# A graph network on one core: indirect fetches that name only the rows a slot can use, in steps of 32

## The chip, the cores and the metric

The kernel runs on one core of a Trainium2 chip. The time is device microseconds of one execution; the figure given for a kernel is the median of several runs. Before the change it is 6249.97 us (three runs: 6262.89, 6249.97 and 6209.29 us).

The engines appear under these names: PE multiplies matrices (PEld loads its weights), DVE is the vector engine, ACT the scalar engine with its activation functions, POOL the general engine, which also issues every indirect DMA here, and SP issues plain DMAs. Each engine runs its own list of instructions in order, and the lists wait for one another through semaphores.

## What is computed

The reference is a chain of eight layers on 3125 nodes with 256 features: four graph layers, each followed by a layer on single nodes. The edge list has 53125 entries (25000 random pairs in both directions and one loop for each node), sorted by destination, so that a node has 17 incoming edges on average. Cut to its frame:

```python
edge_index = jnp.stack([src, dst])
x = x + _L0_gnn_ref(_layernorm(x, axis=-1), edge_index, ...)      # two attention layers
x = x + _L0_ffn_ref(_layernorm(x, axis=-1)[None], ...)[0]
x = x + _L1_gnn_ref(edge_index, _layernorm(x, axis=-1), edge_type_8, ...)   # relational sum
x = x + _L1_ffn_ref(_layernorm(x, axis=-1)[None], ..., L1_ffn_edge_index)[0]  # experts, gates by a graph
x = x + _L2_gnn_ref(_layernorm(x, axis=-1), ...)
x = x + _L2_ffn_ref(_layernorm(x, axis=-1)[None], ...)[0]
x = x + _L3_gnn_ref(_layernorm(x, axis=-1), ..., edge_attr_3, edge_index)   # attention with edge attributes
x = x + _L3_ffn_ref(_layernorm(x, axis=-1)[None], ...)[0]
```

An attention layer computes a score for each edge from the rows of its two nodes, takes a softmax over the edges that enter a node, and adds the source rows with these weights:

```python
m = xl[src] + xr[dst]
logits = jnp.einsum('ehc,hc->eh', jax.nn.leaky_relu(m, NEG_SLOPE), att)
...
out = jax.ops.segment_sum(alpha[:, :, None] * xl[src], dst, num_segments=n_nodes)
```

The gates of the first expert layer come from a small attention layer on a second random graph of 65536 edges, of which those that enter the 3125 nodes matter.

## The kernel before

**Nodes by degree.** The prologue ranks the nodes by their number of incoming edges, largest first (`by_degree`, L1165), and cuts the ranking into NT = 25 groups of P = 128 nodes, one node to a partition. The edges of a group are handled in slots: slot s of a group holds, for each of its 128 nodes, that node's edge number s. How many slots each group gets is fixed when the program is built: `profile` (L1032) works from a Poisson distribution of the degrees and gives KS = 41, 25, 23, 22, 21, 21, 20, ..., 12, 11, 10, in all TOT = 453 slots. OFF holds the first slot of each group. For the second graph KR is KS less one (428 slots, offsets OFFR), since its loops are handled apart. `by_degree` also compares the counted degrees with limits that it writes with memsets into `least` (L1214); if a limit is passed, a flag sends the kernel into a general version for any graph. The limit at slot KS[g] is that at most 128 x g nodes have more edges.

**The gather stages of `quick` (L1414).** Five stages fetch source rows from a table in HBM. For every slot, POOL issues one indirect DMA (`gather`, L1078): 128 indices, one from each partition, and 128 rows into one slot of a tile `gt`. Where a node has fewer edges than the slot number, the index names some other row, and a penalty of -1e30 on the score (`pen`) makes its weight zero; in the relational sum the index names a row of zeros instead (`relz`).

- T1, T2: two attention layers through `gat` (L1650), with rows of 260 and 257 words. A chunk is C4 = 4 slots in one tile; a group has one slot more, for the node's own row, which ACT copies in (L1670). The steps of a chunk are `fetch`, `own`, `add` (DVE adds the destination rows, L1674, ACT takes Abs, L1675) and `score` (DVE, L1680 to L1682), one turn apart; when a group is through, `weigh` (L1601) takes the softmax and forms weighted rows `wv` (DVE, L1637, in T1; ACT, L1635, in T2), which PE adds with an identity matrix (L1623).
- rel: the relational sum through `plain_sum` (L1693), with rows of 256 words. There are no scores: PE adds the fetched rows as they are (L1708). Beside it DVE and POOL sort the second graph, and call `by_degree` for it (L1974).
- gm: the gates, `gates_by_slots` (L2310), with rows of 32 words; a tile holds all slots of a group. Beside it PE, DVE and ACT work on the experts.
- TA: the attention with edge attributes (fetch at L2766), with rows of 264 words; PE encodes the attributes (`enc_ahead`, L2847, and L2800).

**Order.** `pipeline` (L1088) and `in_turns` (L1578) write the order out by hand: each turn issues up to two fetches, as long as a tile is free (14 in `gat` and TA, 12 in `plain_sum`) and the fetch is no more than `lead` chunks ahead (8; 6 in TA), and then one step of each kind for the chunk whose turn it is. Inside one engine nothing overtakes.

Of the kernel before, what the change touches and what calls it, by code (L numbers as in the profile page):

```python
# [11 lines left out]
F32 = mybir.dt.float32  # L12
# [8 lines left out]
P = 128  # L21
D = 256
KD = D // P
N = 3125
NT = (N + P - 1) // P
NP = NT * P
# [1005 lines left out]
def profile():  # L1032


    mean = (E - N) / N
    p = [math.exp(-mean)]
    for i in range(1, 200):
        p.append(p[-1] * mean / i)
    ks = []
    for g in range(NT):  # L1040
        d = 1
        while True:
            tail = max(1.0 - sum(p[:d]), 0.0)
            c = N * tail
            if (c < 1e-3) if g == 0 else (c + 4.0 * math.sqrt(c * (1.0 - tail)) <= P * g):
                break
            d += 1
        ks.append(d)
    return ks


KS = profile()
OFF = [sum(KS[:g]) for g in range(NT)]
TOT = sum(KS)
DC = KS[0] + 3
# [106 lines left out]
        yield 0  # L1162


def by_degree(tc, k, pool, psum, name, cls, total, slots, record, table, bad):  # L1165

    nc = tc.nc
    R, M = cls.shape[0], cls.shape[1]  # L1170
    cls_f = pool.tile([P, DC], F32, name="cls_f")
    nc.gpsimd.iota(cls_f, pattern=[[1, DC]], base=0, channel_multiplier=0, allow_small_or_imprecise_dtypes=True)
    before = pool.tile([P, P], F32, name="before")
    nc.gpsimd.affine_select(out=before, in_=k.ones, pattern=[[1, P]], compare_op=ALU.is_gt,
                            fill=0.0, base=0, channel_multiplier=-1)
    keep = pool.tile([R, DC, M], F32, name="keep")
    nc.gpsimd.memset(keep, 1.0)
    nc.gpsimd.memset(keep[:, :, 0:1], 0.0)
    S = [R, DC, M]
    oh = pool.tile(S, F32, name="oh0")  # L1180
    nc.vector.tensor_tensor(oh, cls_f[:R, :, None].to_broadcast(S), cls[:, None, :].to_broadcast(S), ALU.is_equal)
    yield 0
    pre = pool.tile(S, F32, name="pre")
    nc.vector.tensor_tensor_scan(pre.rearrange("p c t -> p (c t)"), keep.rearrange("p c t -> p (c t)"),
                                 oh.rearrange("p c t -> p (c t)"), 0.0, op0=ALU.mult, op1=ALU.add)
    tot = pool.tile([R, DC], F32, name="tot")
    nc.vector.tensor_copy(tot, pre[:, :, M - 1])
    yield 0
    cps = psum(2 * DC).rearrange("p (s c) -> p s c", s=2)
    nc.tensor.matmul(cps[:, 0, :], k.ones[:R, :], tot, start=True, stop=True)  # L1190
    nc.tensor.matmul(cps[:, 1, :], before[:R, :], tot, start=True, stop=True)
    yield 0
    cum = pool.tile([R, DC], F32, name="cum")
    nc.vector.tensor_tensor_scan(cum, k.ones[:R, :DC], cps[:R, 0, :], 0.0, op0=ALU.mult, op1=ALU.add)
    bb = pool.tile([R, DC], F32, name="bb")
    nc.vector.scalar_tensor_tensor(bb, cum, -1.0, cps[:R, 1, :], op0=ALU.mult, op1=ALU.add)
    nc.vector.tensor_scalar_add(bb, bb, float(total - 1))
    nc.vector.tensor_add(pre, pre, bb[:, :, None].to_broadcast(S))
    yield 0
    nc.vector.tensor_mul(pre, pre, oh)  # L1200
    rank = pool.tile([R, M], F32, name="rank")
    nc.vector.tensor_reduce(rank, pre.rearrange("p c t -> p t c"), AX.X, ALU.add)
    yield 0
    rank_i = pool.tile([R, M], I32, name="rank_i")
    nc.vector.tensor_copy(rank_i, rank)
    nrec = pool.tile([R, M, 4], F32, name="nrec")
    nrec_i = nrec.bitcast(I32)
    nc.vector.memset(nrec[:, :, 3:], 0.0)
    nc.vector.tensor_copy(nrec_i[:, :, 0], record[0])
    nc.vector.tensor_copy(nrec_i[:, :, 1], record[1])  # L1210
    nc.vector.tensor_copy(nrec[:, :, 2], record[2])
    least = pool.tile([R, DC], F32, name="least")
    nc.gpsimd.memset(least, 0.0)
    for g in range(NT - 1, -1, -1):  # L1214
        nc.gpsimd.memset(least[:, slots[g] + 1 : slots[g] + 2], float(total - P * g))
    over = pool.tile([R, DC], F32, name="over")
    nc.vector.tensor_tensor(over, cum, least, ALU.is_lt)
    nc.vector.tensor_reduce(bad[:R, :], over, AX.X, ALU.add)
    yield 0
    for t in range(M):  # L1220
        scatter(tc, name, table, rank_i[:, t : t + 1], nrec[:, t, :])
        for _ in range(4):
            yield 0
# [54 lines left out]
def prologue(tc, a, k):  # L1278
# [8 lines left out]
    with tc.tile_pool(name="pr", bufs=1) as pr, tc.tile_pool(name="prw", bufs=3) as prw, \  # L1287
# [59 lines left out]
        bad = pr.tile([P, 5], F32, name="bad")  # L1347
        nc.vector.memset(bad, 0.0)
        for _ in by_degree(tc, k, pr, lambda n: prp.tile([P, P], F32, name="s_ps", bufs=2)[:, :n], "perm", cls,
                           NP, KS, (n_f, S[:, :NT], deg), k.perm_d, bad[:, 0:1]):  # L1350
            pass


# [60 lines left out]
def quick(ctx: ExitStack, tc: tile.TileContext, a: dict, out: bass.AP, k):  # L1414
# [16 lines left out]
    slot = q.tile([P, KS[0]], F32, name="slot")  # L1431
    nc.gpsimd.iota(slot, pattern=[[1, KS[0]]], base=0, channel_multiplier=0,
                   allow_small_or_imprecise_dtypes=True)
    zeros = q.tile([P, W1], F32, name="zeros")
    nc.vector.memset(zeros, 0.0)
    zero = zeros[0:1, :D]

# [160 lines left out]
    def all_chunks(own=0):  # L1598
        return [(g, c, n, c + n == KS[g] + own) for g in range(NT) for c, n in chunks(g, own)]

    def weigh(pool, psum, g, L, H, tiles, own=0):  # L1601


        K = KS[g] + own
        by_head = L.rearrange("p k h -> p h k")
        nc.vector.tensor_add(L[:, : KS[g], :], L[:, : KS[g], :],
                             pen[:, OFF[g] : OFF[g] + KS[g], None].to_broadcast([P, KS[g], H]))
        mx = pool.tile([P, H], F32, name="mx")
        nc.vector.tensor_reduce(mx, by_head, AX.X, ALU.max)
        if not own:  # L1610
            nc.vector.tensor_scalar_max(mx, mx, -0.5 * BIG)
        nc.vector.tensor_sub(L, L, mx[:, None, :].to_broadcast([P, K, H]))
        nc.scalar.activation(L, L, AF.Exp)
        yield 0
        den = pool.tile([P, H], F32, name="den")
        nc.vector.tensor_reduce(den, by_head, AX.X, ALU.add)
        acc = psum.tile([P, D], F32, name="acc", bufs=2)
        held = []

        def summed():  # L1620
            for c, n, wv in held:
                for s in range(n):
                    nc.tensor.matmul(acc, ident, wv[:, s, :], start=(c + s == 0), stop=(c + s == K - 1))  # L1623
            held.clear()


        todo = list(zip(chunks(g, own), tiles))
        per = 2 if len(todo) > 6 else 1
        for i in range(0, len(todo), per):
            made = []  # L1630
            for (c, n), t in todo[i : i + per]:
                wv = pool.tile([P, C4, D], F32, name="wv", bufs=4)
                if H == 1:
                    for s in range(n):
                        nc.scalar.activation(wv[:, s, :], t[:, s, :D], AF.Copy, scale=L[:, c + s, 0:1])  # L1635
                else:
                    nc.vector.tensor_mul(wv[:, :n, :].rearrange("p s (h c) -> p s h c", h=H),  # L1637
                                         t[:, :n, :D].rearrange("p s (h c) -> p s h c", h=H),
                                         L[:, c : c + n, :, None].to_broadcast([P, n, H, D // H]))
                made.append((c, n, wv))  # L1640
            summed()
            held.extend(made)
            yield len(made)
        summed()
        weighed[g] = acc, den
        yield 0
# [3 lines left out]
    def gat(H, table, own_rows, att, gp, mp, sp, psum, opened, finish, beside=None):  # L1650
# [5 lines left out]
        def fetch(g, c, n, last):  # L1656
# [3 lines left out]
                        st[a_] = SimpleNamespace(R=own_rows(a_), tiles={})  # L1660
            t = st[g].tiles[c] = gp.tile([P, C4, W], F32, name="gt")
            for s in range(n - last):
                gather(nc, t[:, s, :], table, recs_i[:, OFF[g] + c + s, 0:1])

        def own(g, c, n, last):
            if c == 0:
                opened(g)
                st[g].L = sp.tile([P, KS[g] + 1, H], F32, name="L", bufs=4)
# [24 lines left out]
    def plain_sum(table, idx, gp, psum, start, tail, beside=None):  # L1693
# [3 lines left out]
        def fetch(g, c, n, last):  # L1697
            t = tiles[g, c] = gp.tile([P, C4, D], F32, name="gt")
            for s in range(n):
                gather(nc, t[:, s, :], table, idx[:, OFF[g] + c + s : OFF[g] + c + s + 1])  # L1700

        def add(g, c, n, last):
            if c == 0:
# [1 line left out]
                start(accs[g], g)  # L1705
            t = tiles.pop((g, c))
            for s in range(n):
                nc.tensor.matmul(accs[g], ident, t[:, s, :], start=False, stop=(last and s == n - 1))  # L1708
            return 1

        pipeline(tc, all_chunks(), 12, 8, fetch, (add,), lambda g: tail(g, accs.pop(g)), beside, 4)
# [161 lines left out]
    def route_merge(pool, psum, pieces, G):  # L1873
# [69 lines left out]
        for i in range(4):  # L1943
# [27 lines left out]
        cls = pool.tile([RQ, 25], F32, name="rm_cls")  # L1971
        nc.vector.tensor_scalar(cls, deg, 1.0, float(DC - 1), op0=ALU.add, op1=ALU.min)
        nc.vector.tensor_scalar_max(cls, cls, 0.0)
        yield from by_degree(tc, k, pool, psum, "perm2", cls, N, KR, (ids[:RQ, :], at_f[:, :25], deg), perm2_d,  # L1974
                             bad[:, 2:3])
        ps = psum(5)
        nc.tensor.matmul(ps, ones, bad, start=True, stop=True)
# [332 lines left out]
    def gates_by_slots(gc, gp, sp, beside, pieces):  # L2310
# [23 lines left out]
        def fetch(g):  # L2334
            t = tiles[g] = gp.tile([P, KR[g] + 1, GW], F32, name="gt")
            for i in range(KR[g]):
                gather(nc, t[:, i, :], gm, recs2[:, OFFR[g] + i : OFFR[g] + i + 1])
            nc.scalar.copy(t[:, KR[g], :], own[g])

        def score(g):  # L2340
# [381 lines left out]
    with tc.tile_pool(name="ag", bufs=abufs) as gp, tc.tile_pool(name="am", bufs=2) as mp, \  # L2722
# [43 lines left out]
        def fetch(g, c, n, last):  # L2766
            t = gp.tile([P, C4, WA], F32, name="gt")
            tiles.setdefault(g, []).append(t)
            for s in range(n):
                gather(nc, t[:, s, :], TA, recs_i[:, OFF[g] + c + s, 0:1])  # L2770

        def attrs(g, c, n, last):
            if c % SE == 0:
# [71 lines left out]
                ready[2 - j](*seq[i - 1 - j])  # L2845

        def enc_ahead(g, c, n, last):  # L2847
            i = seq.index((g, c, n, last))
            for j, r in enumerate(ready):
                if i + j < len(seq):  # L2850
# [169 lines left out]
```

## Time and profile before

| | |
|---|---|
| median of three runs | 6249.97 us |
| profiled execution, its own time | 6249.48 us |
| its span, first to last instruction | 6247.7 us |
| mean granted TensorE clock | 0.758 |
| chain that ended last | PE 14%, issue 13%, POOL 5%, DVE 4%, DMA 2% of the span |

The costliest groups that touch the gathers, with their busy time and the mean of one:

| group | count | busy us | mean ns |
|---|---|---|---|
| L1079 POOL indirect DMA, T1 and T2 | 906 | 1013.0 | 1118 |
| L1079 POOL indirect DMA, gm | 428 | 468.1 | 1094 |
| L1079 POOL indirect DMA, TA | 453 | 462.9 | 1022 |
| L1079 POOL indirect DMA, rel | 453 | 441.9 | 975 |
| L1623 PE, adding weighted rows | 2818 | 915.0 | 485 |
| L1708 PE, adding rows in rel | 906 | 324.0 | 490 |
| L1674 DVE, adding destination rows | 258 | 297.1 | 1152 |
| L1675 ACT, Abs | 258 | 256.4 | 994 |

Busy time on POOL is the time in which it prepares the DMA; the data land later. A group's idle time names what the engine waited for before it: "issue" means that the profile shows nothing it waited for. PE adds in fp32 with two passes, so L1708 has two records for each slot. A window of the profile gives the busy time of each engine between two times.

### The profile page before, as it was taken

The page shows a single profiled execution, that of the slowest core. Times are in us where ns is not written, and L with a number is a line of the kernel's source. Part 1 is how long each engine was busy: PE and PEld are TensorE (multiplying, and loading weights), DVE is VectorE, ACT ScalarE, POOL GpSimd, SP SyncE. Part 2 cuts the span into 40 slices and gives each one's busy share as a digit, 9 for nine tenths or more (in the row PEclk, how much of TensorE's full clock was granted, in tenths as well). Part 3 has the DMA queues.
Part 4 walks back from the last instruction along what each step waited for, and adds up shares of the span by engine and source line. Part 5 has one row for each costly group of instructions (what it writes and reads, how often), then busy time and mean ns, then how long its engine had stood idle before and what let it go on. Part 6 is the DMA issues. An engine that isn't in the chain of part 4 may idle for free. (4 is left out here: it accounts for less than half of the span.)

```text
span 6247.7 us, 45320 instructions
## 1 busy us (share of the span) xinstructions
PE 3803.4 (61%) x14067; PEld 2490.4 (40%) x14119; DVE 3126.3 (50%) x6081; ACT 1220.8 (20%) x2574; POOL 3144.9 (50%) x3123
## 2 busy tenths in 40 slices
PE   2344543455598844635286630799695788838885
PEld 1233332333355423424154320465352344426664
DVE  4588878898874345601153324423214677840001
ACT  1222212445622100000043320211021000002221
POOL 3677774667773276675456563210106566631112
PEclk9666766677799956657698765899756777869998
DMA  3533442333312233222243223332242233324444
GB/s 123 142 103 99 108 110 81 94 91 104 91 23 84 112 91 93 78 75 56 60 135 80 57 54 98 105 107 98 71 131 87 78 88 85 89 83 140 159 156 132
DMA packets 356485, 601.24 MB, mean 96 GB/s; under 512 B 109648, under 2 KB 252858, under 8 KB 352898
## 3 DMA queue, kind: packets, MB, share of 16 engines
q0 software_dynamic: 131472, 329.19, 19.7%
q1 hardware_dynamic: 202233, 246.71, 12.3%
q10 hardware_dynamic: 22518, 22.24, 1.1%
q8 instruction: 116, 1.90, 0.1%
q14 instruction: 146, 1.20, 0.1%
HBM read 458.81 MB, written 142.98 MB: 96 GB/s over the span
## 5 line engine op out<-in xcount | busy, mean ns | idle before, releaser
L1623 PE MATMUL acc<-wv,ident 128*128 128x256 f32 x2818 | 915.0, 485 | 601.4 <-ACT wv L1635 259.3
L1079 POOL DMA_INDIRECT gt<-T,recs x906 | 1013.0, 1118 | 354.5 <-issue 247.8
L1623 PEld LDWEIGHTS acc<-wv,ident 128*128 128x128 f32 x2818 | 659.9, 245 | 860.4 <-ACT wv L1635 290.0
L1079 POOL DMA_INDIRECT gt<-TA,recs x453 | 462.9, 1022 | 250.6 <-issue 130.3
L1079 POOL DMA_INDIRECT gt<-gm,recs x428 | 468.1, 1094 | 172.3 <-issue 130.0
L1079 POOL DMA_INDIRECT gt<-rel,relz x453 | 441.9, 975 | 205.9 <-issue 128.2
L1708 PE MATMUL acc<-gt,ident 128*128 128x256 f32 x906 | 324.0, 490 | 207.8 <-issue 163.0
L2569 PE MATMUL acc<-XNT,adj_g 128*128 128x512 bf16 x1198 | 404.1, 386 | 42.1 <-ACT XNT L2561 42.1
L2800 PE MATMUL e_ps<-EW,att 32*128 32x512 f32 (+7 forms) x466 | 307.2, 787 | 130.6 <-ACT att L2790 65.5
L1675 ACT ACTIVATE m<-m 128x1024 f32<-128x1024 f32 (+2 forms) x258 | 256.4, 994 | 579.7 <-DVE m L1674 351.5
L2572 PE MATMUL acc<-F,adj_g 128*128 128x256 bf16 x1250 | 344.1, 276 | 8.9 <-DVE F L2562 6.2
L1674 DVE TENSOR_TENSOR m<-gt,R 128x1028 f32<-128x1028 f32 (+4 forms) x258 | 297.1, 1152 | 78.3 <-DMA gt<-T,recs 76.2
L1708 PEld LDWEIGHTS acc<-gt,ident 128*128 128x128 f32 x906 | 208.3, 243 | 305.0 <-issue 191.6
L1083 POOL DMA_INDIRECT top_out<-ys,to x64 | 62.9, 984 | 513.7 <-DVE ys L2935 456.1
L2921 PE MATMUL fh_ps<-xt,w 128*128 128x256 f32 x1024 | 266.8, 399 | 75.8 <-ACT ht L2923 73.9
L1680 DVE TENSOR_TENSOR m<-m,att 128x1024 f32<-128x1024 f32 (+2 forms) x258 | 294.2, 1140 | 27.8 <-issue 27.8
L1681 DVE TENSOR_REDUCE L<-m 128x4 f32<-128x1024 f32 (+4 forms) x258 | 294.3, 1141 | 13.4 <-remote 5.5
L1637 DVE TENSOR_TENSOR wv<-gt,L 128x1024 f32<-128x1024 f32 (+3 forms) x252 | 285.3, 1137 | 21.5 <-issue 9.1
L2441 PE MATMUL x_ps<-XNT,x_w 128*128 128x512 f32 (+1 forms) x448 | 232.4, 654 | 95.5 <-ACT x_h L2443 65.6
L2462 DVE TENSOR_TENSOR x_y<-x_o,x_b 128x512 f32<-128x512 f32 (+1 forms) x52 | 34.4, 669 | 427.4 <-remote 161.0
L2921 PEld LDWEIGHTS fh_ps<-xt,w 128*128 128x128 f32 x1024 | 187.7, 193 | 150.0 <-ACT ht L2923 126.7
L2933 PE MATMUL fo_ps<-w,ht 128*128 128x256 f32 x1024 | 226.3, 379 | 0.0
(562 smaller groups left out, 6600.5 us busy)
## 6 DMA issues: line engine op xcount, KB each, us to landing
w<-in_L_ffn_W_dram SPq DMA_DIRECT2D x64, 1024.0 KB
adj_g<-adj SPq DMA_DIRECT2D x50, 800.0 KB
adj<-em_a SPq DMA_DIRECT2D x25, 800.0 KB
gt<-T,recs POOLq DMA_INDIRECT x906
y<-each_d SPq DMA_DIRECT2D x25, 512.0 KB
each_d<-x_y SPq DMA_DIRECT2D x24, 512.0 KB
R<-rr SPq DMA_DIRECT2D x25, 388.0 KB
top_in<-zeros SPq DMA_DIRECT2D x8, 1028.0 KB
```

Source lines behind the costliest of these rows:

```text
L1079: return nc.gpsimd.indirect_dma_start(out=out_, out_offset=None, in_=table, in_offset=index(idx))
L1623: nc.tensor.matmul(acc, ident, wv[:, s, :], start=(c + s == 0), stop=(c + s == K - 1))
L1637: nc.vector.tensor_mul(wv[:, :n, :].rearrange("p s (h c) -> p s h c", h=H), t[:, :n, :D].rearrange("p s (h c) -> p s h c", h=H), L[:, c : ...
L1674: nc.vector.tensor_add(m[:, :n, :], st[g].tiles[c][:, :n, :], st[g].R[:, 1:2, :].to_broadcast([P, n, W]))
L1675: nc.scalar.activation(m[:, :n, :D], m[:, :n, :D], AF.Abs)
L1680: nc.vector.tensor_mul(m[:, :n, :D], m[:, :n, :D], att[:, None, :].to_broadcast([P, n, D]))
L1681: nc.vector.tensor_reduce(L, m[:, :n, :D].rearrange("p s (h c) -> p s h c", h=H), AX.X, ALU.add)
L1708: nc.tensor.matmul(accs[g], ident, t[:, s, :], start=False, stop=(last and s == n - 1))
L2569: nc.tensor.matmul(acc.rearrange("p s d -> p (s d)"), A[:, b, :], F12[:, b, :, :].rearrange("p s d -> p (s d)"), start=(b == 0), stop=Fals ...
L2572: nc.tensor.matmul(acc[:, 0, :], A[:, b, :], F3_[:, b, :], start=False, stop=(b == NT - 1), skip_group_check=True)
L2800: nc.tensor.matmul(e_ps[:, :z, :].rearrange("p s d -> p (s d)"), att, EW[: att.shape[0], s0 : s0 + z, :].rearrange("p s d -> p (s d)"), st ...
L2921: nc.tensor.matmul(ps[:, i, :], ld[j][1][:, c, (f_ + i) * P : (f_ + i + 1) * P], xt[j][:, c, :], start=(c == 0), stop=(c == KD - 1))
```

## The change

`profile` also returns MOST: for each slot s a bound on the number of nodes with more than s edges, five standard deviations and three nodes above the expected count. `rows_at` turns it into the number of rows of group g that can use slot s, rounded up to 32. The four fetches name only these rows. In the three attention stages and in gm, `no_rows` lets ACT copy zeros into the other rows, in pieces that start at row 32, 64 or 96, since the steps after it read the whole tile; in the relational sum the product takes only the named rows. `by_degree` takes MOST as its limits, slot by slot, in place of the limit at each KS[g]. The tile `zeros` grows from 257 to 264 columns.

```diff
+    most = []
+    for s in range(ks[0] + 1):
+        tail = max(1.0 - sum(p[:s]), 0.0)
+        c = N * tail
+        most.append(min(math.ceil(c + 5.0 * math.sqrt(c * (1.0 - tail))) + 3,
+                        P * min([g for g in range(NT) if ks[g] <= s], default=NT)))
+    return ks, most
...
+def rows_at(g, s):
+    return min(P, -(-(MOST[s] - P * g) // 32) * 32)
...
-    for g in range(NT - 1, -1, -1):
-        nc.gpsimd.memset(least[:, slots[g] + 1 : slots[g] + 2], float(total - P * g))
+    for s in range(len(most)):
+        nc.gpsimd.memset(least[:, s + 1 : s + 2], float(max(total - most[s], 0)))
...
+    def no_rows(t, g, c, n):
+        for s in range(n):
+            r = rows_at(g, c + s)
+            while r < P:
+                e = P if r in (0, 64) else r + 32
+                nc.scalar.copy(t[r:e, s, :], zeros[r:e, : t.shape[2]])
+                r = e
...
             for s in range(n - last):
-                gather(nc, t[:, s, :], table, recs_i[:, OFF[g] + c + s, 0:1])
+                r = rows_at(g, c + s)
+                gather(nc, t[:r, s, :], table, recs_i[:r, OFF[g] + c + s, 0:1])
 
         def own(g, c, n, last):
+            no_rows(st[g].tiles[c], g, c, n - last)
...
-                nc.tensor.matmul(accs[g], ident, t[:, s, :], start=False, stop=(last and s == n - 1))
+                r = rows_at(g, c + s)
+                nc.tensor.matmul(accs[g], ident[:r, :], t[:r, s, :], start=False, stop=(last and s == n - 1))
...
-                gather(nc, t[:, i, :], gm, recs2[:, OFFR[g] + i : OFFR[g] + i + 1])
+                r, o = rows_at(g, i + 1), OFFR[g] + i
+                gather(nc, t[:r, i, :], gm, recs2[:r, o : o + 1])
+            no_rows(t, g, 1, KR[g])
             nc.scalar.copy(t[:, KR[g], :], own[g])
...
         def enc_ahead(g, c, n, last):
+            no_rows(tiles[g][c // C4], g, c, n)
```

The fetches of the relational sum and of TA change as the first one does. `rows_at` gives 128 for 420 of the 453 slots.

More of the change, by code (lines that the diff above doesn't have):

```diff
@@ L1048, in profile @@
         ks.append(d)
-    return ks
-KS = profile()
+    most = []
[5 more added lines that the diff above has]
+    return ks, most
+KS, MOST = profile()
+def rows_at(g, s):
+    return min(P, -(-(MOST[s] - P * g) // 32) * 32)
 OFF = [sum(KS[:g]) for g in range(NT)]
@@ L1162, in staggered, with by_degree @@
         yield 0
-def by_degree(tc, k, pool, psum, name, cls, total, slots, record, table, bad):
+def by_degree(tc, k, pool, psum, name, cls, total, most, record, table, bad):
     nc = tc.nc
@@ L1349, in prologue @@
         for _ in by_degree(tc, k, pr, lambda n: prp.tile([P, P], F32, name="s_ps", bufs=2)[:, :n], "perm", cls,
-                           NP, KS, (n_f, S[:, :NT], deg), k.perm_d, bad[:, 0:1]):
+                           NP, MOST, (n_f, S[:, :NT], deg), k.perm_d, bad[:, 0:1]):
             pass
@@ L1433, in quick @@
                    allow_small_or_imprecise_dtypes=True)
-    zeros = q.tile([P, W1], F32, name="zeros")
+    zeros = q.tile([P, D + 8], F32, name="zeros")
     nc.vector.memset(zeros, 0.0)
@@ L1699, in fetch @@
             for s in range(n):
-                gather(nc, t[:, s, :], table, idx[:, OFF[g] + c + s : OFF[g] + c + s + 1])
+                r, o = rows_at(g, c + s), OFF[g] + c + s
+                gather(nc, t[:r, s, :], table, idx[:r, o : o + 1])
         def add(g, c, n, last):
@@ L1973, in route_merge @@
         nc.vector.tensor_scalar_max(cls, cls, 0.0)
-        yield from by_degree(tc, k, pool, psum, "perm2", cls, N, KR, (ids[:RQ, :], at_f[:, :25], deg), perm2_d,
+        yield from by_degree(tc, k, pool, psum, "perm2", cls, N, MOST[1:], (ids[:RQ, :], at_f[:, :25], deg), perm2_d,
                              bad[:, 2:3])
@@ L2769, in fetch @@
             for s in range(n):
-                gather(nc, t[:, s, :], TA, recs_i[:, OFF[g] + c + s, 0:1])
+                r = rows_at(g, c + s)
+                gather(nc, t[:r, s, :], TA, recs_i[:r, OFF[g] + c + s, 0:1])
         def attrs(g, c, n, last):
```

## The prediction

> **What bounds the kernel now.** I read the page first, then the five gather stages by windows, then the gathers themselves by tile, then POOL in order of time.
>
> ```profile
> PE 3803.4 (61%) x14067; PEld 2490.4 (40%) x14119; DVE 3126.3 (50%) x6081; ACT 1220.8 (20%) x2574; POOL 3144.9 (50%) x3123
> ```
>
> No engine is busy throughout, and the chain that ended last has no piece at all before 2920 us, so it cannot say what bounds the first three gather stages. The windows can. Each runs from the first gather of a stage to its last one: first attention layer (table T1), second (T2), the relational sum (rel), the routing gates (gm), the attribute attention (TA).
>
> ```profile
> core 0: us, PE busy (x) PEld busy (x) DVE busy (x) ACT busy (x) POOL busy (x), PEclk, DMA share, GB/s
> 197.00:940.00 743.00, 309.33 (x1016) 236.12 (x1016) 589.60 (x809) 165.08 (x258) 571.21 (x508) 0.68 0.40 106
> 1019.00:1711.00 692.00, 322.96 (x936) 225.67 (x936) 607.54 (x988) 332.51 (x653) 498.66 (x455) 0.69 0.35 96
> 2166.00:2922.00 756.00, 377.28 (x1164) 256.97 (x1164) 300.36 (x723) 14.19 (x55) 504.42 (x542) 0.64 0.30 81
> 2923.00:3844.00 921.00, 460.92 (x1751) 286.64 (x1751) 294.70 (x549) 230.73 (x483) 545.76 (x506) 0.73 0.27 69
> 4767.00:5479.00 712.00, 552.74 (x1393) 290.02 (x1392) 493.33 (x903) 43.76 (x171) 462.82 (x453) 0.73 0.32 86
> ```
>
> POOL looks 50 to 77% busy here, but the order of time shows that it cannot go faster between two gathers:
>
> ```profile
> 300.26 0.95 POOL L1079 DMA_INDIRECT gt<-T,recs  x1 [0.30 <-issue]
> 301.52 0.95 POOL L1079 DMA_INDIRECT gt<-T,recs  x1 [0.30 <-issue]
> 302.77 0.96 POOL L1079 DMA_INDIRECT gt<-T,recs  x1 [0.30 <-issue]
> ```
>
> Every gather is followed by 0.30 us of issue, so one costs 1.25 us. Busy time plus 0.30 us for each instruction gives POOL's true occupation: T1 571.2 + 508 x 0.30 = 723.6 of 743 us (97%), T2 635 of 692 (92%), rel 667 of 756 (88%), gm 698 of 921 (76%), TA 599 of 712 (84%). T1 is bound by POOL; in T2 DVE is at 88% too, and in TA POOL waits 111.9 us for DVE's wv to free buffers. I count a POOL microsecond as 0.97 on the path in T1, 0.88 in rel, 0.5 in T2, gm and TA (a choice): 3.35 stages. The upper bound is the occupations themselves, 4.37 stages.
>
> **What a gather of fewer rows costs.** This is the whole question, since the diff keeps every gather and only shortens some. By the row rule in the code, 33 of 453 slots in T1, T2, rel and TA each are shortened: 13 to 32 rows, 15 to 64, 5 to 96; in gm it is 32 (13, 14, 5). Fifteen lie in group 0 (slots 26 to 40), ten are all of group 24, eight are single last slots. That is 164 of 2240 gathers, and 4 x 2368 + 2304 = 11776 of 286720 rows (4.1%), or 92 full gathers.
>
> ```profile
> L1079 POOL DMA_INDIRECT gt<-T,recs x906: 947/953/2747, 197.2 to 1710.0; - x182
> L1079 POOL DMA_INDIRECT gt<-gm,recs x428: 938/944/3649, 2927.0 to 3818.3; - x143
> L1083 POOL DMA_INDIRECT rel<-hx,PR x25: 961/961/1005, 1941.2 to 2161.2; - x25
> ...
> L1083 POOL DMA_INDIRECT perm_d<-nrec,rank_i x25: 963/967/1067, 96.4 to 127.0; - x25
> ...
> L1083 POOL DMA_INDIRECT perm_d<-nrec,rank_i x25: 1208/1211/1319, 2622.6 to 2790.2; - x25
> ```
>
> At 128 rows the median is 0.94 to 0.97 us whether a row is 16 bytes (the first perm_d), 128 bytes (gm) or 8 KB (the scatter to rel). Bytes cost POOL nothing, so smaller transfers save nothing by being smaller. Whether rows cost anything has one witness: the same scatter of 16-byte records has 128 rows in the prologue (0.967 us) and 125 rows later (1.211 us). Fewer rows, 0.244 us more. No row shows 32, 64 or 96. So the bounds are, from below, time in proportion to rows: 2368/128 = 18.5 gathers x 0.95 = 17.6 us of POOL a stage (gm 17.0); from above, every short one pays the 125-row surcharge: 33 x 0.244 = 8.1 us a stage. I take zero, the 128-row price, because the one pair that varies rows speaks against proportion. On the path the ends are -17.6 x 3.35 = -58 us (-76 by occupations) and +27 us (+35).
>
> The Trainium skill has a rule against the change: DMA: Bandwidth & Descriptors, "Anatomy of one DMA — SWDGE (gpsimd) path", calls descriptor generation "small, variable" and says that many descriptors can be emitted before their cost shows. Its section "Why a DMA increments its semaphore by 16 and not by 1" spreads a transfer over the largest number of DMA engines up to 16 that divides its rows: 16 for 128, 96, 64 and 32 rows, but 5 for 125. Read so, 25 instead of 8 rows an engine cost 0.244 us, an estimate of 14 ns a step: a 32-row gather would save 0.09 us, a stage 2.1 us, and the sum would be 7 us lower than mine.
>
> **The added copies.** The unread rows of the tile are filled by ACT, since the sums that follow read all 128: 46 copies of zeros in T1, T2 and TA, 45 in gm. The nearest rows are L1670, 128x260 at 391 ns, and L2338, 128x32 at 202 ns: 138 x 0.39 + 45 x 0.20 = 63 us of ACT in all. The instruction order of PE and SP is unchanged, DVE's too; its adds of the affected chunks wait for ACT besides the gathers. In group 0 a full chunk of 32-row slots brings 8 copies, 3.1 us, ahead of an Abs of 1.06 us: 4.2 us on ACT, while POOL needs 4 x 1.25 = 5.0 us for the chunk's gathers. ACT is at 22% in T1, 2% in rel (which needs no copies), 25% in gm, 6% in TA: nothing there. In T2 it is at 48%, and near the end (33 to 35 busy us of 50) it makes wv too, so group 24's 11 copies (4.3 us) queue ahead of Abs and wv, for which POOL already waits 41.0 us through full buffers. Bounds 0 to 4.3 us; I take 2. If the cover were gone everywhere, the cost is 63 us.
>
> **The rest.** The limits of by_degree are written by 42 and 41 memsets instead of 25 each, on POOL: 25 took 2.00 us at 2616 us, so 17 more are 1.4 us in the prologue, at 3.6 us, where the scatters behind them start at 96 us after a 21 us wait for DVE: nothing. In rel 16 more are 1.3 us, POOL's scatters and gathers queue behind them: +1.3 us. The wider zeros memset, 273 ns before, gains 7 of 257 columns: nothing. The short matmuls of the relational sum keep 256 columns (490 ns); PE is at 50% there, and its K=32 products elsewhere (L2800, 813 ns for 512 columns) show no penalty worth counting: zero, bounds -3 to +3 us.
>
> **Sum.** 0 + 2 + 1.3 = +3 us on the profiled execution's 6249.5 us, which stands 0.5 us under the median of the three runs (6250.0): 6252 to 6253 us.
>
> **The rivals.** *Rows are what a gather costs.* For it: no row of the trace has fewer than 125 rows, so nothing refutes it below that; against it: the 125-row scatter. Time 6249.5 + 3 - 58 = 6195 us, by occupations 6176. *A short gather leaves the quick path,* as 125 rows do: each takes 1.21 us or more, first where POOL is bound, in T1. At 0.244 us extra the time is 6280 us (6288); it is slower by over 1% only from about 62 / (164 x 0.67) = 0.56 us extra per gather, which no row shows. *ACT's copies stand in the way:* up to 6249.5 + 63 = 6313 us; against it is ACT's 20%. *The change doesn't do what it says:* tighter limits could send the kernel into its general version. Counted on the reference's inputs, no limit is passed (the closest: 2872 nodes use slot 11, 2944 are allowed), so the chance is under 0.01 and I price it only as far slower.
>
> **How the numbers follow.** A measurement of this kernel tells about 1% (62 us) from no change; its own three runs lie from 41 us under to 13 us over the median. Flat price 0.62; proportion 0.22; surcharge 0.11; ACT 0.04; general version 0.01. Faster by over 1% (under 6187): a third of the proportional case and 0.01 of the flat one for the spread of runs, 0.08. Slower (over 6312): 0.04 of the surcharge, 0.01 of ACT, 0.01 general, 0.01 flat: 0.07. The rest, 0.85, is within 1%. The range takes in most of the proportional case and the surcharge at its upper weight: 6185 to 6290 us.
>
> **What would show it.** The forms of L1079 by rows: 32-row gathers near 0.95 us prove the flat price, 0.24 us proportion, 1.2 us the surcharge. T1 between its first and last gather should stay at 743 us within a few; group 0's adds there, which the order of time has 5.2 us apart (L1674, 218.5 to 255.2 us), should stay so. ACT's new line should total about 63 us with few waiters; if DVE's add in T1 (L1674 before) waits for ACT instead of the gathers, the copies are not hidden. My forecast is wrong if short gathers cost much under 0.7 us.

## The result, and the profile after

The changed kernel takes 6222.6 us, the kernel before 6236.7 us (medians of twelve runs each). The ratio is 0.9994, with a 95% interval from 0.9973 to 1.0015: no change that can be measured, 4 us faster by the ratio with room from 17 us faster to 9 us slower (the medians alone are 14 us apart). Medians and ratios in this document leave out two slow runs, one of 6994.8 us of rel_32 and one of 8236.2 us of the kernel before. The forecast was 6252 us in a range of 6185 to 6290 us. The profiled execution has a span of 6209.8 us, 38 us under the one of before; the runs of either kernel spread over 55 us and more, so this difference says nothing.

The busy times of the page, to be held against the first line shown of before:

```profile
PE 3789.5 (61%) x14067; PEld 2488.7 (40%) x14119; DVE 3126.4 (50%) x6081; ACT 1286.8 (21%) x2757; POOL 3149.5 (51%) x3156
```

ACT has 183 instructions and 66 us more: the copies, whose own line adds up to 63.2 us. POOL has 33 more (the limits of by_degree) and no less work than before. The five gather stages by windows, from the first gather of each to its last (the columns are those of before; the window of the gates also takes in the fetches of each group's own rows):

```profile
196.00:939.00 743.00, 319.47 (x1016) 242.56 (x1016) 589.62 (x809) 179.44 (x292) 568.04 (x506) 0.67 0.40 104
1013.00:1725.00 712.00, 329.81 (x984) 231.67 (x983) 614.26 (x1001) 357.95 (x716) 502.41 (x456) 0.69 0.33 91
2176.00:2934.00 758.00, 386.10 (x1164) 261.34 (x1164) 299.81 (x723) 14.29 (x55) 501.76 (x558) 0.64 0.28 77
2939.00:3808.00 869.00, 450.90 (x1751) 284.82 (x1751) 294.34 (x548) 240.60 (x528) 552.32 (x501) 0.75 0.28 72
4735.00:5443.00 708.00, 535.77 (x1384) 283.50 (x1383) 491.40 (x897) 62.75 (x217) 457.81 (x453) 0.74 0.31 83
```

T1 lasts 743 us as before. T2 is 20 us longer, the gates 52 us shorter, and neither need belong to the change: two later kernels, on the second chip of the experiments, that left T1 and T2 as they were had 1531 and 1527 us from the first gather of T1 to the last of T2, this one has 1528.5 and the profile of before 1512.8; the gates lasted 867 to 881 us, first slot gather to last, in three later kernels where nothing was changed in them, 891 in the profile of before and 844 here. The 23 us by which the gates here lie under those kernels have no cause that a run shows. At the end of T2, where the prediction saw the copies queue ahead of ACT's wv, POOL waits 53.4 us for wv, after 41.0 us before and 47.6 to 51.0 us in three later kernels without copies. That is 2 to 6 us more than in those three, and no run shows whether they lie on the path.

The gathers themselves, by tile (duration: least, median, most):

```profile
L1093 POOL DMA_INDIRECT gt<-T,recs x906: 867/953/3178, 196.5 to 1725.0; - x182
L1093 POOL DMA_INDIRECT gt<-rel,relz x453: 867/946/2983, 2176.7 to 2897.4; - x151
```

The least was 947 and 940 ns. The short gathers are the new least, and group 0's 32-row slots in T1 show them one after another in POOL's order of time:

```profile
248.07 0.87 POOL L1093 DMA_INDIRECT gt<-T,recs  x1 [0.30 <-issue]
249.25 0.87 POOL L1093 DMA_INDIRECT gt<-T,recs  x1 [0.30 <-issue]
```

A quarter of the rows costs 0.87 instead of 0.95 us, and the 0.30 us of issue stays. Matched by order with the slots, 64 rows take 0.91 us and 96 rows 0.93 (medians in the relational sum: 872, 911, 928 and 946 ns for 32, 64, 96 and 128 rows). So 33 short gathers save 13 x 0.074 + 15 x 0.035 + 5 x 0.018 = 1.6 us of POOL a stage, of some 440 to 570.

The adds that wait for these gathers and for the copies (DVE, T1), first two of before, then four of now:

```profile
249.88 1.24 DVE L1674 TENSOR_TENSOR m<-gt,R 128x1040 f32<-128x1040 f32 x1 [1.38 <-DMA gt<-T,recs]
255.16 1.24 DVE L1674 TENSOR_TENSOR m<-gt,R 128x1040 f32<-128x1040 f32 x1 [1.44 <-DMA gt<-T,recs]
```

```profile
241.06 1.24 DVE L1700 TENSOR_TENSOR m<-gt,R 128x1040 f32<-128x1040 f32 x1 [1.16 <-DMA gt<-T,recs]
245.78 1.24 DVE L1700 TENSOR_TENSOR m<-gt,R 128x1040 f32<-128x1040 f32 x1 [0.88 <-ACT gt L1622]
250.60 1.24 DVE L1700 TENSOR_TENSOR m<-gt,R 128x1040 f32<-128x1040 f32 x1 [0.98 <-DMA gt<-T,recs]
255.30 1.24 DVE L1700 TENSOR_TENSOR m<-gt,R 128x1040 f32<-128x1040 f32 x1 [0.86 <-DMA gt<-T,recs]
```

They are 4.7 to 4.8 us apart, not 5.2 to 5.3 as before, and three of the four wait for the gathers, one for ACT. The copies' own line, with all who waited for it:

```profile
L1622 ACT COPY gt<-zeros x183: 209/404/411, 233.2 to 5443.1; 64x260 f32<-64x260 f32 x28, 64x257 f32<-64x257 f32 x28, 64x264 f32<-64x264 f32 x28, 64x32 f32<-64x32 f32 x27
...
  PEld small L2815: 8.6, 1
  DVE m L1700: 0.9, 1
  PEld e_ps L2831: 0.7, 1
  POOL gt L1093: 0.6, 2
```

In all 11 us of waiting, 8.6 of it once on PE at TA, where the stage did not grow by it (707 us between first and last gather, 711 before).

### The profile page after: what moved, and what is told of

Its sections match the earlier page's. It is cut to its first block, busy times and chain, and to the rows that moved or that the text cites. A ratio compares the mean times of both kernels' runs of the same rounds, so it can differ in the third digit from the quotient of the medians.

```text
span 6209.8 us, 45581 instructions
## 1 busy us (share of the span) xinstructions
PE 3789.5 (61%) x14067; PEld 2488.7 (40%) x14119; DVE 3126.4 (50%) x6081; ACT 1286.8 (21%) x2757; POOL 3149.5 (51%) x3156
## 3 DMA queue, kind: packets, MB, share of 16 engines
q0 software_dynamic: 129680, 319.08, 19.3%
## 5 line engine op out<-in xcount | busy, mean ns | idle before, releaser
L1736 PE MATMUL acc<-gt,ident 128*128 128x256 f32 (+2 forms) x906 | 327.1, 492 | 216.8 <-issue 172.9
L1736 PEld LDWEIGHTS acc<-gt,ident 128*128 128x128 f32 (+2 forms) x906 | 208.3, 242 | 317.1 <-issue 213.1
L2485 PE MATMUL x_o<-x_w,x_h 128*128 128x256 f32 x800 | 205.6, 404 | 34.7 <-issue 20.7
```

The lines of the kernel that those rows point to most:

```text
L1736: nc.tensor.matmul(accs[g], ident[:r, :], t[:r, s, :], start=False, stop=(last and s == n - 1))
```

## The experiments

Theory: a gather costs POOL nearly the same whatever its rows, the copies are hidden, and a POOL microsecond has a weight in each stage that the prediction chose by hand. Rivals: rows set the price (something hid the gain); short gathers pay a surcharge; the copies give back what the gathers gain. Twelve kernels ran, on three chips (m_rows, the two kernels with copies and rel_32 on the first, the four with added memsets on the second, the rest on the third). The kernel before took 5801.4 us on the first, 6234.0 us on the second and 5797.6 us on the third, so each ratio is taken against the kernel before on the same chip.

**The price of a gather by rows** (m_rows). A kernel of its own; it computes no layer, only gathers rows of 256 and then of 32 words:

```python
ROWS = (128, 127, 126, 125, 124, 120, 112, 96, 80, 64, 48, 32, 16, 8)
...
            for r in ROWS:
                for s in range(S):
                    nc.gpsimd.indirect_dma_start(out=t[r][:r, s, :], out_offset=None, in_=table,
                                                 in_offset=bass.IndirectOffsetOnAxis(ap=idx[:r, s : s + 1], axis=0))
```

> This kernel computes none of the layers: it only fetches rows of x, 8 gathers for each number of rows from 128 down to 8, once with rows of 256 words and once with 32, and writes a tile of sums. In the changed kernel a gather took 0.867 us for 32 rows, 0.91 for 64, 0.93 for 96 and 0.945 for 128, and the scatter of 125 rows took 1.21. Theory (flat price, less a small step for every row of a multiple of 16): 112 rows 0.94, 80 rows 0.92, 48 rows 0.89, 16 rows 0.85, 8 rows 0.85. What 124, 125, 126 and 127 rows cost it leaves open; 125 should be 1.21 again. Rival (a count that is no multiple of 32 leaves the quick path): 127, 126, 125, 124, 120, 112, 80, 48, 16 and 8 rows all take about 1.2 us. The Trainium skill, DMA: Bandwidth & Descriptors, section on why a DMA increments its semaphore by 16, spreads a transfer over the largest divisor of its rows up to 16. By that and 14 ns a row of one engine, an estimate, 127 rows would take 2.7 us, 126 rows 0.97, 125 rows 1.20, 124 rows 1.28, 120 rows 0.95.

The lines by tile; the tile's second letter gives the rows, here 128, 127, 125, 124, 64 and 32:

```profile
L31 POOL DMA_INDIRECT wa<-in_x_dram,idx x8: 942/945/959, 11.2 to 19.9; - x8
L31 POOL DMA_INDIRECT wb<-in_x_dram,idx x8: 2547/2548/2560, 21.2 to 41.2; - x8
L31 POOL DMA_INDIRECT wd<-in_x_dram,idx x8: 1195/1202/1207, 54.4 to 64.9; - x8
L31 POOL DMA_INDIRECT we<-in_x_dram,idx x8: 1290/1292/1297, 66.4 to 77.6; - x8
L31 POOL DMA_INDIRECT wj<-in_x_dram,idx x8: 904/906/911, 112.8 to 121.3; - x8
L31 POOL DMA_INDIRECT wl<-in_x_dram,idx x8: 867/872/872, 132.0 to 140.2; - x8
```

Over multiples of 16 the price falls gently: 945 ns at 128 rows, 920 at 96, 906 at 64, 872 at 32, 847 at 16 (and 860 at 8). Rows of 128 bytes have the same medians within 4 ns for every count. Other counts are no matter of "fewer": 127 rows cost 2548 ns, 126 992, 125 1202, 124 1292, 120 981. The proportional rival falls, and so does the one that every count off the multiples of 32 pays 1.2 us: the surcharge is real but belongs to 125 and its like, none of which the change uses. A gather of 127 rows also lands 10.4 us after its issue (median), one of 125 rows after 4.2 and one of 128 after 2.7; over how many DMA engines each was spread, no view here shows. The rule of the Trainium skill that the prediction weighed (DMA: Bandwidth & Descriptors, "Why a DMA increments its semaphore by 16 and not by 1") agrees: the largest divisor up to 16 is 1 for 127, 14 for 126, 5 for 125, 4 for 124 and 15 for 120. The estimate above from it and the first profile's pair, 2.7, 0.97, 1.20, 1.28 and 0.95 us, lies within 6% of all five.

**The copies without the short gathers** (copies_only). Every gather at 128 rows; ACT writes the same zeros into a tile that nobody reads:

```diff
-                nc.scalar.copy(t[r:e, s, :], zeros[r:e, : t.shape[2]])
+                nc.scalar.copy(spare[r:e, : min(t.shape[2], 240)], zeros[r:e, : min(t.shape[2], 240)])
...
-                gather(nc, t[:r, s, :], table, recs_i[:r, OFF[g] + c + s, 0:1])
+                gather(nc, t[:, s, :], table, recs_i[:, OFF[g] + c + s, 0:1])
```

> The changed kernel with all gathers at 128 rows again and the zeros written to a spare tile, so ACT has its 183 copies (about 63 us) and POOL has gained nothing. Theory of the prediction (copies hidden beside POOL's gathers): the time of the kernel before within 4 us, ratio 1.000 to 1.001, and nobody waits for the copies' line. Rival (the shorter gathers gain and the copies give it back): slower than before by at least the 7 us that 0.08 us a short gather is worth, and waits of other engines on ACT in group 0 of T1, T2 and TA.

5804.2 us, ratio 1.0002 (0.9991 to 1.0012): 63 us of ACT are worth between 5 us less and 7 us more. Its copies write another tile, so that no add waits for them (PE waits 7.1 us for ACT behind them in TA); ACT's time is hidden, and the wait of the adds is seen only in the profile after (0.9 us).

**Four times the copies** (copies_x4), on the changed kernel:

```diff
-                nc.scalar.copy(t[r:e, s, :], zeros[r:e, : t.shape[2]])
+                for _ in range(4):
+                    nc.scalar.copy(t[r:e, s, :], zeros[r:e, : t.shape[2]])
```

> The changed kernel with every copy of zeros made four times: 189 us more on ACT. Theory (hidden as long as ACT keeps up): in group 0 a full chunk of 32-row slots now costs ACT 32 x 0.405 + 1.06 = 14 us while POOL needs 4.7 us, so T1 and T2 each fall behind by up to 30 us in three chunks; POOL runs up to 8 chunks ahead meanwhile, so part of it comes back: 10 to 50 us slower in all, most of it in T1 and T2. Rival (the copies lie on the path already): three more times 63 us, 150 to 190 us slower, spread over all groups that have copies. If nothing is felt at all (under 10 us), ACT has far more room than I gave it.

5842.9 us, 1.0072 (1.0057 to 1.0087): 42 us for 191 us more of ACT (254.0 for 63.2), and DVE's adds wait 52.0 us for the copies, where they waited 0.9. So the cover is not endless, but the first 63 us lie under it.

**All gathers of the relational sum at 32 rows** (rel_32), on the kernel before; the messages to the other 96 nodes of each group are left out:

```diff
-                gather(nc, t[:, s, :], table, idx[:, OFF[g] + c + s : OFF[g] + c + s + 1])
+                gather(nc, t[:32, s, :], table, idx[:32, OFF[g] + c + s : OFF[g] + c + s + 1])
...
-                nc.tensor.matmul(accs[g], ident, t[:, s, :], start=False, stop=(last and s == n - 1))
+                nc.tensor.matmul(accs[g], ident[:32, :], t[:32, s, :], start=False, stop=(last and s == n - 1))
```

> The kernel before, with all 453 gathers of the relational sum at 32 rows and the product over those rows alone; the messages to the other 96 nodes of each group are left out. Theory (a gather costs POOL 0.08 us less at 32 rows, and 0.88 of POOL's time in rel is on the path): 453 x 0.08 = 36 us less of POOL, 32 us off the stage of 756 us, total ratio 0.995. Rival (time in proportion to the rows): 453 x 0.71 = 320 us of POOL, the stage falls by 200 us and more. Rival (POOL is not what sets the stage): the stage stays at 750 to 760 us.

5777.2 us, 0.9956 (0.9941 to 0.9971): by the ratio 25.5 us faster for three quarters of the stage's rows and bytes. POOL got 453 x 0.074 = 33.5 us less, and the stage, 649 us between first and last gather in copies_only, became 616 us. Were rows the price, 453 x 0.71 = 320 us of POOL would have gone.

**The same stage at 125 rows** (rel_125): the same edit with 125 for 32.

> The kernel before with all 453 fetches of the relational sum, and its products, at 125 rows; the messages to the last three nodes of each group are left out. The gather by itself took 1.20 us at 125 rows against 0.945 at 128, so POOL gets 453 x 0.256 = 116 us more. By the weight that the 32-row run of this stage gave (25.5 us won for 33.5 us of POOL, 0.76) the kernel is 88 us slower, by my 0.88 of the prediction 102 us, by 1 116 us. The rival, that the surcharge belongs to the scatter of by_degree and not to a gather in this stage, gives 0 or a small gain. Bytes (2.3% fewer rows) give a gain of some 10 us at most if rows are the price.

5916.5 us, 1.0208 (1.0191 to 1.0225): 121 us slower (111 to 130), with 2% fewer rows. The stage's gathers by tile, in copies_only (128 rows) and here:

```profile
L1093 POOL DMA_INDIRECT gt<-rel,relz x453: 942/946/2987, 2112.7 to 2761.9; - x151
```

```profile
L1079 POOL DMA_INDIRECT gt<-rel,relz x453: 1191/1203/3220, 2102.2 to 2865.3; - x151
```

649 us became 763 (copies_only ran on the first chip, which is as quick as the third). POOL got 453 x 0.257 = 116 us more, a weight of 1.04 (0.95 to 1.12). From the 32-row run the weight is 0.76 with room from 0.5 to 1.0; the two agree near 1.

**What a POOL microsecond is worth in the other stages** (pool_T1, pool_T2, pool_gm, pool_TA). The kernel before, with two memsets behind each gather of one stage (the cut shows the call for T1 and T2; `extra` names the stage):

```diff
+    padt = q.tile([P, 120], F32, name="padt")
+    extra = ("T1",)
+
+    def more(stage):
+        if stage in extra:
+            nc.gpsimd.memset(padt, 0.0)
+            nc.gpsimd.memset(padt, 0.0)
...
                 gather(nc, t[:, s, :], table, recs_i[:, OFF[g] + c + s, 0:1])
+                more("T1" if H > 1 else "T2")
```

> The kernel before, with two memsets of 128x120 on POOL behind each of the 453 gathers of the first attention layer, and nothing else. They say what a POOL microsecond is worth in that stage. The added pitch from one gather to the next is read from the profile (two small memsets partly lie in the 0.30 us of issue, so 0.1 to 0.4 us is my estimate from the 80 ns of by_degree's memsets). My weight for T1 (0.97) gives 0.97 x 453 = 439 us for each microsecond of added pitch: 44 us at 0.1, 132 us at 0.3. The rival that POOL is not what bounds T1 (DVE is busy for 590 of its 743 us) gives under half of that.

> The same in the second attention layer. My weight of 0.5 gives 0.5 x 453 = 227 us for each microsecond of added pitch: 23 us at 0.1, 68 us at 0.3. The rival, that POOL's occupation of 92% is the weight, gives 417 us for each microsecond: 42 and 125 us. That DVE alone bounds T2 gives about 0.

> The same behind the 428 gathers of the gates. My weight of 0.5 gives 214 us for each microsecond of added pitch: 21 us at 0.1, 64 us at 0.3. By the occupation (76%) 325 us: 33 and 98 us. If the experts that run beside it set the stage's end, 0.

> The same behind the 453 gathers of the attention with attributes. My weight of 0.5 gives 227 us for each microsecond of added pitch: 23 us at 0.1, 68 us at 0.3. By the occupation (84%) 381 us: 38 and 114 us. If the encoder's products on PE and DVE's wv set the pace, for which POOL waited 111.9 us in the kernel before, that wait shrinks first and the cost is near 0.

POOL's order of time in the gates of pool_gm shows the added pitch, 1.57 us from gather to gather for 1.25:

```profile
3300.11 0.95 POOL L1079 DMA_INDIRECT gt<-gm,recs  x1 [0.16 <-issue]
3301.06 0.21 POOL L1440 MEMSET padt<- 128x120 f32 x1
3301.33 0.20 POOL L1441 MEMSET padt<- 128x120 f32 x1
3301.68 0.95 POOL L1079 DMA_INDIRECT gt<-gm,recs  x1 [0.15 <-issue]
```

Added POOL time below is the memsets with the gaps before them, plus what the stage's gathers and their issue gaps gained or lost against the other kernels on this chip:

| stage | memsets + gaps | gathers, issue | added POOL us | kernel, us | weight (95%) | my choice | occupation |
|---|---|---|---|---|---|---|---|
| T1 | 186.9 + 26.3 | +31.3, -31.8 | 213 | +189 (1.0303) | 0.89 (0.81 to 0.96) | 0.97 | 0.97 |
| T2 | 188.0 + 26.3 | -2.0, -7.9 | 204 | +129 (1.0207) | 0.63 (0.55 to 0.71) | 0.5 | 0.92 |
| gm | 175.7 + 24.7 | +31.1, -55.3 | 176 | -2 (0.9997) | 0 (-0.07 to 0.05) | 0.5 | 0.76 |
| TA | 186.0 + 26.3 | +28.4, -23.2 | 217 | +65 (1.0105) | 0.30 (0.18 to 0.42) | 0.5 | 0.84 |

That the memsets slow DVE instead of holding POOL back can be ruled out: T1's adds take 1241 ns in pool_T1 and 1239 ns in before, but wait 276.3 us for their gathers, against 72.3 us in pool_TA, where T1 is as before.

The zero of the gates can be read in their groups. In pool_TA, where the gates are as before (idle time of the engine behind the second bar):

```profile
L1079 POOL DMA_INDIRECT gt<-gm,recs x428 | 467.2, 1092 | 210.0 <-issue 127.5 <-DVE pen L2356 71.3 <-DVE L L2363 4.3
L1079 POOL DMA_INDIRECT own<-gm,PR x25 | 28.1, 1125 | 63.7 <-DVE L L2357 56.2 <-issue 6.9 <-DVE gln_s L76 0.3
L1083 POOL DMA_INDIRECT gd<-gates_o,own_at x25 | 26.5, 1060 | 67.5 <-DVE gates_o L2379 61.1 <-issue 5.8 <-DMA recs<-csr_d,PR 0.6
```

and in pool_gm:

```profile
L1079 POOL DMA_INDIRECT gt<-gm,recs x428 | 497.7, 1163 | 82.1 <-issue 73.0 <-DVE L L2363 3.4 <-DMA recs<-csr_d,PR 1.4
L1079 POOL DMA_INDIRECT own<-gm,PR x25 | 25.5, 1022 | 9.5 <-issue 7.5 <-DVE x_y L2473 2.0
L1083 POOL DMA_INDIRECT gd<-gates_o,own_at x25 | 27.1, 1086 | 20.6 <-DVE gates_o L2379 13.7 <-issue 5.1 <-DMA recs<-csr_d,PR 1.5
```

POOL waited 71.3, 56.2 and 61.1 us for DVE there; the first two waits went and the third fell to 13.7 us, together 175 us, as much as was added, and the stage lasted 868 us, against 870 us. In TA it is the same in part. Unchanged, in pool_T1:

```profile
L1079 POOL DMA_INDIRECT gt<-TA,recs x453 | 454.9, 1004 | 261.7 <-issue 127.8 <-DVE wv L1645 109.1 <-DVE L L2837 19.4
```

and in pool_TA:

```profile
L1079 POOL DMA_INDIRECT gt<-TA,recs x453 | 484.0, 1069 | 120.8 <-issue 105.2 <-DVE L L2825 4.6 <-DVE X L2846 3.1
```

The wait for wv to free buffers, 109.1 us, is gone. The stage grew by 100 us between its first and last gather (814 against 714), and 36 us of that came back in the work behind the last gather, which took 730 us instead of 766.

**Fewer gathers by stacking** (packed). In the relational sum alone, twelve of group 0's 32-row slots go four to a gather, two 64-row slots of group 0 and eight of group 24 two to a gather (w slots of r rows, m such gathers to a strip); the indices are stacked on DVE, and PE folds the rows back. The eleven short slots of the stage that are left are fetched short (32 to 96 rows), which by the prices above is worth 0.4 us; the other stages are as before.

```diff
+            if m:
+                strips.append((g, ss[0], m, w, r, col))
+                us += [(True, col + i, P, r) for i in range(m)]
...
+            for j in range(w):
+                nc.vector.tensor_copy(relp[j * r : (j + 1) * r, col : col + m], from_[:, :, j])
...
+                w, o = (fold[:, 0:64] if r == 64 else fold[:, 64:96], accs[g][:r]) if packed else (ident[:k, :], accs[g])
+                nc.tensor.matmul(o, w, t[:k, s, :], start=False, stop=(last and s == n - 1))
```

> The number of gathers instead of their rows, in the relational sum alone: twelve of group 0's 32-row slots go into 3 gathers of 128 rows (four slots stacked), two of its 64-row slots into one and eight of group 24's into four; PE adds the stacked rows with a folded identity. 439 gathers instead of 453; all other stages as before. If the number counts, POOL gets 14 x 1.25 = 17.5 us less, at a weight of 0.76 13 us, less some 2 us for stacking the indices on DVE: 11 us faster, 0.998. If only rows count (the rival), nothing is won by stacking beyond what 14 x 128 - the rows saved by the short fetches would give: under 2 us.

5768.4 us, 0.9947 (0.9933 to 0.9962): 31 us faster (22 to 39), more than expected.

```profile
L1113 POOL DMA_INDIRECT gt<-rel,relz x431: 877/946/2987, 2111.6 to 2735.4; - x144
...
L1113 POOL DMA_INDIRECT gt<-rel,relp x8: 946/957/1007, 2106.5 to 2734.2; - x8
```

The eight stacked gathers cost what any gather of 128 rows costs. The stage lasts 629 us, 20 us less than the 649 of copies_only on the first chip, for 17.5 us of POOL taken out (and 28 of PE's 906 products, with PE waiting 136.0 us for gathers in copies_only). The other 2 to 19 us lie outside the stage, and no run places them.

**Fewer slots** (fewer). The kernel before with 446 slots, of a narrower margin over the expected degrees; more graphs would then need the general version:

```diff
-            if (c < 1e-3) if g == 0 else (c + 4.0 * math.sqrt(c * (1.0 - tail)) <= P * g):
+            if (c < 0.05) if g == 0 else (c + 3.0 * math.sqrt(c * (1.0 - tail)) <= P * g):
```

> The kernel before with 446 slots instead of 453: the slots of a group come from three standard deviations instead of four, and group 0's from an expected 0.05 nodes beyond them instead of 0.001 (36 slots instead of 41), so that more graphs would need the general version. 7 gathers fewer in each of the five stages, 8.75 us of POOL each. With the weights measured in the runs before (0.91 for T1, 0.66 for T2, 0.76 for the relational sum, 0 for the gates, 0.30 for TA, together 2.63): 23 us faster, 0.996. With the prediction's 3.35: 29 us. If fetches are not on the path: 0.

5758.3 us, 0.9929 (0.9914 to 0.9944): 41 us faster (32 to 50), where 23 were expected. (The text above works with 0.91 and 0.66 for T1 and T2; the table's 0.89 and 0.63 change its sum by under 1 us.) Four kernels on the two quick chips (copies_only, rel_32, rel_125, packed) left the gathers of T1, T2 and TA at 128 rows and their number as it was. Between first and last gather T1 and T2 together take 1459 to 1466 us there and 1445 here, 14 to 21 us less for 17.5 us of POOL; TA takes 605 to 613 there and 595 here, 10 to 18 less for 8.75; the relational sum takes 649 in copies_only and 639 here, 10 less for 8.75; the gates lose no more than 9. That is a weight of about 1 in each but the gates, TA too, where the second chip had shown 0.30. It is not the gathers' alone: a slot that is dropped spares DVE, ACT and PE their work for it as well, and no run parts the two. What is different about TA can be seen in copies_only, on a chip as quick as this one:

```profile
L1093 POOL DMA_INDIRECT gt<-TA,recs x453 | 469.0, 1035 | 139.4 <-issue 123.0 <-DVE m L2842 2.7 <-DMA gt<-TA,recs 2.7
```

There POOL waits 16 us for others in TA, against 134 us on the second chip, the stage takes 606 us, and POOL with its issue is on 592 of them, so hardly any slack is left to use up first. The weight that I had carried over for TA from the second chip was too small here, as far as this run can tell.

**Both together** (best): 446 slots, and 438 gathers for them in the relational sum.

> Both of the last two edits together: 446 slots, and in the relational sum 438 gathers for them (four 32-row slots and two pairs fewer than in the packed kernel, since group 0 has lost five slots). 23 us for the slots and 8 x 1.25 x 0.76 = 8 us for the stacking, less 2 us on DVE: 29 us faster, 0.995.

5731.0 us, 0.9880 (0.9865 to 0.9895): 70 us faster (61 to 78), the fastest kernel of the study. The two edits alone gave 41 and 31; five slots that one drops are among those that the other stacks (eight 32-row slots fewer are stacked here than in packed, and all five pairs), so 41 + 31 x 8/14 = 59 would be their sum, just under the measured range.

## Why the prediction was right

The measured time alone tells little: the range of 6185 to 6290 us took in two of the rivals as well, 6195 us if rows set the price and 6280 us with the surcharge. The ratio, 17 us faster to 9 us slower, leaves out both, and the experiments show why.

*The price of a short gather* was taken as flat: 0.95 us whatever the rows. The mechanism is right, the size was 8% off at 32 rows: 0.872 us alone and 0.87 in the kernel, 1.6 us less a stage. The estimate drawn from the Trainium skill (DMA: Bandwidth & Descriptors, "Why a DMA increments its semaphore by 16 and not by 1"), 0.09 us a gather and 2.1 us a stage, was nearer than mine. The proportional bound (0.24 us, 58 us less) is refuted by m_rows and by rel_32, the upper bound (0.244 us more) holds for 125 rows, as rel_125 shows, and not for 32, 64 or 96. The witness that I used, a scatter of 125 rows, was a true one about 125 and said nothing of fewer rows; that the zero chosen on its word came within 1.6 us a stage was in part luck.

*The weights*, a choice of mine, summed to 3.35. Measured on the second chip, with 1 for the relational sum from the third, they are 0.89 + 0.63 + 1.0 + 0 + 0.30 = 2.8. The relational sum's 1.0 comes from the quick chips, where POOL waits 21.5 us for others in it (copies_only); in the profile of before it waits 77.7 us, so its weight there may be smaller, which was not tried. The occupations, my upper bound, are near the weight in T1 and under it in the relational sum (0.88 against 1.04), but far over it in T2, the gates and, on the second chip, TA. The gates were the largest miss: 76% of occupation, 0 on the path, since 71, 56 and 61 us of waits for DVE lay on POOL as slack.

*The copies* were put at 63 us of ACT, hidden, 2 us on the path of 0 to 4.3. They are 63.2 us by their line, and copies_only bounds what their ACT time costs at 7 us. Even 191 us more of them cost 42 us, not 191, so part of the cover holds beyond them.

*The limits of by_degree and the short products* (+1.3 us, 0 +- 3) were not tried alone; the relational sum has 721 us between first and last gather after 718.5, which agrees with them but is one execution each.

*The sum* was +3 us. With the measured price and weights, and the other two terms as predicted, it is -1.6 x 2.8 + 2 + 1.3 = -1.2 us; measured are -4 us with room from -17 to +9. The runs of the two kernels cannot tell these apart, only the experiments on the terms can. Two slips in the working change nothing: POOL's busy shares in the five windows are 59 to 77%, not 50 to 77, and 17.6 x 3.35 is 59, not 58.

*What would show it:* T1 stayed at 743 us and ACT's line came at 63.2 us with few waiters. Two signs missed: the 32-row gathers came at 0.87 and not 0.95, and so group 0's adds at 4.7 to 4.8 us, not 5.2; one add did wait for ACT, for 0.9 us.

So the change moves little for a plain reason: it saves rows and bytes (10 MB, 329.19 to 319.08 on POOL's queue), and neither is what the stages wait for. What T1, T2, the relational sum and TA wait for, each by its weight, is the number of gathers, 1.25 us each, which it leaves as it was.

## What to carry to other kernels

Where the order of time shows an indirect fetch as a fixed time plus a fixed gap, cut the number of fetches, not their rows: 14 gathers fewer won 31 us, 20 of them in the stage itself, and 4% fewer rows nothing that can be measured. Keep the row count of what remains at a multiple of 16: one row less than 128 cost 2.55 us instead of 0.95. Before an occupied engine is counted as the path, look for its waits on others in that stage: they are used up first, and how large they are can differ from chip to chip (134 us in TA on one chip, 16 on another).

## What the hardware showed beside this

- The price of a gather jumps with the row count and not in order: 945 ns at 128, 2548 at 127, 992 at 126, 1202 at 125, 1292 at 124, 981 at 120.
- The kernel before takes 5801, 6234 and 5798 us on the three chips. In TA the granted clock was 0.73 in the first profile and 0.79 in copies_only, and the products of L2800 took 815 and 753 ns; but in the relational sum the clocks are alike (0.64 and 0.65) and the stage is 69 us shorter (718.5 and 649), 56 of them in POOL's waits for others (77.7 and 21.5). What makes the chip of the first profile slower there was not tried.
